# A graph layer's edge gather: 19 chunks loaded row by row from the sync engine, and gathers issued 17 instead of 26 ahead

## The chip, the cores and the metric

The kernel runs on one core of a Trainium2 chip. A core has five engines that run side by side, each through its own list of instructions in order: TensorE (PE in the profile: matmuls; PEld: its weight loads), VectorE (DVE), ScalarE (ACT), GpSimd (POOL) and SyncE (SP). They wait for each other by semaphores. DMA transfers are issued by an engine's sequencer (SP, ACT) or by POOL, and run on 16 DMA engines. SP does no arithmetic: here it issues DMAs and loads registers.

The metric is the device time of one execution in microseconds (us). The kernel before was timed in three runs.

## The reference

A pre-norm graph layer over 12500 nodes of 128 values and 200000 edges, of which the rows `dst` are sorted:

```python
h = jnp.maximum(_layernorm(x, axis=-1), 0.0)
msgs = z[src]                                        # z is h: 200000 rows of 128
agg = jax.ops.segment_sum(msgs, dst, num_segments=n)
deg = jax.ops.segment_sum(jnp.ones((src.shape[0],), z.dtype), dst, num_segments=n)
agg = agg / jnp.maximum(deg, 1.0)[:, None]
h = jax.nn.relu(agg @ Wg + z @ Ws + bg)
h = jnp.tanh(h @ W1 + b1)                            # 128 -> 512
h = jnp.tanh(h @ W2 + b2)                            # 512 -> 512
return h @ W3 + b3                                   # and x is added
```

So for each edge a row of 512 bytes has to be fetched from the normalized table by a number known only at run time, and the rows of edges with the same destination have to be summed.

## The kernel before

**Tables.** A first stage normalizes x and leaves the result twice: in HBM as `htab` (a row a node) and in SBUF, transposed, as `tab` (a column a node). The edges are cut into 1563 chunks of 128. A chunk is summed by one matmul: the 128 fetched rows are the weights, a one-hot matrix of 24 columns (`oh`, made on DVE by `onehot`, line 541) says which destination each row belongs to, and the result is added into a PSUM bank `agg` (or `edge`, for chunks across two blocks of nodes). Float32 matmuls stand in the trace as two records each. After each block of 512 nodes the layer's dense part (`h`, `w`, `pm`) runs on PE and ACT, in pieces between the chunks.

**Four sources of a chunk's rows.**

- *Raw*: ten groups of 8 chunks (`raw`, line 102) are gathered from x itself at the very start, before `htab` is there, by 80 indirect DMAs of POOL (line 217), and normalized later on DVE.
- *Gathered*: 1323 chunks are fetched by one indirect DMA each, issued by POOL (`gather`, line 455), into the pool `rows_in` of AHEAD = 26 buffers. Gather number j + 26 goes into the buffer of number j, so POOL waits there until PE has used chunk number j.
- *ACT's pairs*: 72 chunks (`column_copies`, line 492) are put together in SBUF by ACT: 64 small instructions a chunk, each combining two columns of `tab`, addressed by registers that a TENSOR_LOAD fills from the table `places` (16 at a time). PE then transposes the result (`turn`, line 511) and ACT copies it to `turned`.
- *DVE's pairs*: 88 chunks, in the same way on DVE (`column_pairs`, line 501).

Which chunk goes to whom is set in lines 128 to 139: every fourth chunk (3, 7, 11, ...) from 30 on that is not raw is a slot, and slots are dealt out by shares (SHARES, ENDS), each claimant gathering a fraction of a slot at each step, from a starting credit of 0.5.

**Order.** The program is written out chunk by chunk (line 918 on) in one order for all engines. `behind` counts the gathered chunks passed so far. `load_times` gives, in that count, where pieces of ACT's and DVE's loads are written. SP's list holds, in program order: the loads of `nearby` (98 windows of destination bytes, one each 14 chunks, written 5 windows ahead of their use in `tallied` on DVE; 6 buffers), the loads of x (`xb`, one a block) and the stores of the result. Further dependences (`last`, `newest`) keep DVE's pairs and tallies in the written order.

Of the kernel before, what the change touches and what calls it, by code (L numbers as in the profile page):

```python
# [22 lines left out]
F32 = mybir.dt.float32  # L23
BF16 = mybir.dt.bfloat16
I32 = mybir.dt.int32
# [6 lines left out]
P = 128  # L32
# [5 lines left out]
NRAW = 10  # L38
RAW0 = 256
STEP = 112  # L40
AHEAD = 26
LATE, SOON = 28, 14
LEAD = 24
QUICK = 1312
# [36 lines left out]
def windowed(ctx, tc, x, src, dst, Wg, Ws, bg, W1, b1, W2, b2, W3, b3, out, flag):  # L81
# [46 lines left out]
    lanes = ([], [])  # L128
    slots = [c for c in range(AT, NCH, EVERY) if FROM <= c < max(ENDS) and not raw(c)]
    within = [sum(c < end for c in slots) for end in ENDS]  # L130
    owed = [0.5] * 3
    for c in slots:
        shares = [n / k * (c < end) for n, k, end in zip(SHARES, within, ENDS)]
        owed = [o + n for o, n in zip(owed, [*shares, 1 - sum(shares)])]
        kind = max(range(3), key=lambda k: owed[k])
        owed[kind] -= 1
        if kind < 2:
            lanes[kind].append(c)
    apart = sum(lanes, [])

# [101 lines left out]
    places = const.tile([NROW, CPR // EVERY, P], I32, name="places")  # L242
# [39 lines left out]
    with tc.tile_pool(name="ln", bufs=2) as ln:  # L282

        def indices(name, a, pad, keep):
# [7 lines left out]
            nc.scalar.dma_start(r[FULL : FULL + 1, :REST], a[FULL * ROW : E].rearrange("(p e) -> p e", p=1))  # L292
            if name == "src":
                some = r.rearrange("r (q p) -> r q p", p=P)[:, AT::EVERY]
                nc.vector.tensor_scalar(
                    places.rearrange("r q (i t) -> r q t i", t=2), some.rearrange("r q (t i) -> r q t i", t=2),
                    4.0, float(TAB_AT), op0=ALU.mult, op1=ALU.add,
                )
            else:
                r8 = sp.tile([NROW, ROW], U8, name="r8")  # L300
                nc.scalar.copy(r8, r.bitcast(U8).rearrange("r (e b) -> r e b", b=4)[:, :, 0])
                end = ahead_of + NROW * ROW
                nc.scalar.dma_start(bytes_at[ahead_of:end].rearrange("(r e) -> r e", e=ROW), r8)
                past = sp.tile([1, max(ahead_of, past_end)], U8, name="past")
                nc.vector.memset(past, PAST)
                nc.scalar.dma_start(bytes_at[:ahead_of].rearrange("(o e) -> o e", o=1), past[:, :ahead_of])
                nc.scalar.dma_start(bytes_at[end:].rearrange("(o e) -> o e", o=1), past[:, :past_end])
# [144 lines left out]
    def sp_dma(*a):  # L452
        tc.keep_in_program_order(nc.sync.dma_start(*a))
# [8 lines left out]


    def offsets(lane, c, p0):
        r, q = divmod(c, CPR)
        kind = (mybir.EngineType.Activation, mybir.EngineType.DVE)[lane]
        loads, vs = nc.values_load_multi_w_load_instructions(  # L467
            places[r : r + 1, q // EVERY, p0 : p0 + LOADS], engines=[kind], min_val=TAB_AT,
            max_val=TAB_AT + (N - 1) * 4,
            skip_runtime_bounds_check_because="src holds rows of x, as the indirect DMAs take it to",  # L470
        )
        for ld in loads:
            if lane and last:
# [5 lines left out]
        vs = [v.with_bounds(min_val=TAB_AT, max_val=TAB_AT + (N - 1) * 4, guaranteed_mod_val=0, out_of_modulus=4) for v in vs]  # L479
        return enumerate(vs, p0)  # L480

    columns, last = {}, []

    def two(lane, c, p0):

        by_pair = columns[c].rearrange("p (t i) -> p i t", t=2)
        at_v = dict(offsets(lane, c, p0))
        for p in range(p0, p0 + LOADS, 2):
            a, b = (tab[:, bass.ds((at_v[q] - TAB_AT) // 4, 1)] for q in (p, p + 1))
            yield p, by_pair[:, p // 2], a, b  # L490

    def column_copies():
        for c in lanes[0]:
            columns[c] = ed.tile([P, P], F32, name="cols1", bufs=4)
            for p0 in range(0, P, LOADS):
                for p, to, a, b in two(0, c, p0):
                    act.activation(to, both_first, AF.Identity, bias=b, scale=a)
                    if (p + 2) % TOGETHER == 0:
                        yield

    def column_pairs():
        for c in lanes[1]:
            columns[c] = ed.tile([P, P], F32, name="cols2", bufs=6)
            for p0 in range(0, P, LOADS):
                for p, to, a, b in two(1, c, p0):
                    last[:] = [tc.keep_in_program_order(nc.vector.scalar_tensor_tensor(  # L506
                        to, first_only, a, b.to_broadcast([P, 2]), op0=ALU.mult, op1=ALU.subtract
                    ))]
                yield

    def turn(c):

        pt, both = ps_m.tile([P, 4, P], F32, name="pm"), columns.pop(c)
        pe.transpose(pt[:, 0, :], both, ident)
        r = ed.tile([P, D], F32, name="turned", bufs=6)
        act.activation(r, pt[:, 0, :], AF.Copy, scale=-1.0 if c in lanes[0] else 1.0)
        rows_t[c] = r


# [21 lines left out]
    def onehot(g):  # L541
        k = min(GRP, NCH - g * GRP)
        is_raw = raw(g * GRP)
        w = W_RAW if is_raw else W
        oh = ed.tile([P, GRP, W_RAW], F32, name="ohr", bufs=1) if is_raw else oh_bufs[g % OHS]
        newest[:] = [nc.vector.tensor_tensor(  # L546
            oh[:, :k, :w], lane[:, None, :w].to_broadcast([P, k, w]),
            dloc[:, g * GRP : g * GRP + k][:, :, None].to_broadcast([P, k, w]), op=ALU.is_equal,
        )]
        for c in range(g * GRP, g * GRP + k):  # L550
            if c in lanes[0] or c in lanes[1]:
# [217 lines left out]

    def costs(b):  # L770
        n = blocks[b][1]
        return n, 4 * (n / 2400 + 0.003), 0.5 + n / 1200 + (BEHIND if at < lanes[0][-1] else 0)

    def wide(b):

# [100 lines left out]
    def load_times(lane):  # L876
        use = [sum(o < c for o in order) for c in lanes[lane]]
        if not use:
            return
        step = (use[-1] - use[0]) // max(1, len(use) - 1)  # L880
        use = [max(FROM - 46 + MARGIN, use[0] - step), *use]
        some = LOADS if lane else TOGETHER
        for i in range(len(lanes[lane])):
            for k in range(P // some):
                yield max(FROM - 30, use[i] + (use[i + 1] - use[i]) * k * some // P - (MARGIN + GRP if lane else MARGIN))

    loading = [
        (loads, list(load_times(i))) for i, loads in enumerate((column_copies(), column_pairs()))
    ]
    turns = sorted((max(1, sum(o < c for o in order) - MARGIN // 2), c) for c in apart)  # L890
    work, done, nxt, behind = [], 0, 0, 0
    ngrp = -(-NCH // GRP)
    now = at = 0
# [24 lines left out]
    for c in range(NCH):  # L918
# [12 lines left out]
                factors(stats_raw)  # L931

        if c % (GRP // 2) == 0 and g + 2 < ngrp:
            copies, times = loading[1]
            while times and times[0] <= behind:
                times.pop(0)
                next(copies, 0)
# [423 lines left out]
```

## Time and profile before

| | us |
|---|---|
| three runs | 1783.35, 1785.84, 1782.18; median 1783.35 |
| the profiled execution | 1784.42 |
| its span, first to last instruction | 1782.2 |
| POOL busy in the span | 1331.8 (75%) |
| ACT busy | 1538.4 (86%) |
| PE busy | 1387.7 (78%) |
| DVE busy | 1177.0 (66%) |

Busy shares don't count the register, branch, semaphore and DMA-issuing instructions of an engine's sequencer, so SP has no busy time at all, and an engine can be behind without being at 100%. The waits are read by what ended an idle stretch ("<-"); a wait put down to "issue" is one for which the profile shows no semaphore.

### The profile page before, as it was taken

The page shows a single profiled execution, that of the slowest core. Times are in us where ns is not written, and L with a number is a line of the kernel's source. Part 1 is how long each engine was busy: PE and PEld are TensorE (multiplying, and loading weights), DVE is VectorE, ACT ScalarE, POOL GpSimd, SP SyncE. Part 2 cuts the span into 40 slices and gives each one's busy share as a digit, 9 for nine tenths or more (in the row PEclk, how much of TensorE's full clock was granted, in tenths as well). Part 3 has the DMA queues.
Part 4 walks back from the last instruction along what each step waited for, and adds up shares of the span by engine and source line. Part 5 has one row for each costly group of instructions (what it writes and reads, how often), then busy time and mean ns, then how long its engine had stood idle before and what let it go on. Part 6 is the DMA issues. An engine that isn't in the chain of part 4 may idle for free.

```text
span 1782.2 us, 27816 instructions
## 1 busy us (share of the span) xinstructions
PE 1387.7 (78%) x5426; PEld 927.2 (52%) x5426; DVE 1177.0 (66%) x6620; ACT 1538.4 (86%) x5189; POOL 1331.8 (75%) x1412
## 2 busy tenths in 40 slices
PE   1345554799798887878888888888898899879897
PEld 1334444466465555545555545555555555555577
DVE  7979987786567767567575766667757567565200
ACT  2478977999999999999899999999999999996222
POOL 7777777777777777777777777777777777777774
PEclk9999999866877887887776888778786788888898
DMA  8832222222222222222222222222222222222221
GB/s 206 238 91 56 56 56 66 68 60 72 58 73 70 71 62 70 72 59 70 71 60 70 73 60 69 73 59 71 71 60 70 71 57 73 71 66 71 59 63 38
DMA packets 116384, 131.36 MB, mean 74 GB/s; under 512 B 29463, under 2 KB 92819, under 8 KB 116008
## 3 DMA queue, kind: packets, MB, share of 16 engines
q0 software_dynamic: 44896, 92.04, 19.9%
q1 hardware_dynamic: 68030, 33.94, 7.1%
q10 hardware_dynamic: 3276, 3.51, 0.7%
q14 instruction: 136, 1.11, 0.2%
q8 instruction: 46, 0.75, 0.2%
HBM read 116.37 MB, written 13.03 MB: 73 GB/s over the span
## 4 chain that ended last, share of the span: by engine, by line
PE 29%; ACT 25%; DMA 20%; issue 10%; DVE 6%; ACTq 4%; POOL 3%; DVEq 0%; POOLq 0%
ACT cols L524 22%; DMA rows<-htab,scol 20%; PE pm L447 19%; PE agg L447 6%; ACTq L467 4%; DVE cols L506 3%; POOL rows L457 3%; ACT h L524 2%; PE edge L447 2%; PE pm L450 1%; DVE h L280 1%; DVEq L467 0%; ACT turned L524 0%; PE pm L385 0%; DVE nearby L593 0%
## 5 line engine op out<-in xcount | busy, mean ns | idle before, releaser
L457 POOL DMA_INDIRECT rows<-htab,scol x1323 | 1252.7, 947 | 403.2 <-issue 214.6
L524 ACT ACTIVATE cols<-both_first,tab 128x2 f32<-128x2 f32 x4608 | 1337.4, 420 | 11.9 <-issue 8.0
L506 DVE SCALAR_TENSOR_TENSOR cols<-first_only,tab 128x2 f32<-128x2 f32 x5632 | 813.0, 217 | 284.9 <-issue 283.5
L447 PE MATMUL pm<-h,w 128*128 128x512 f32 (+4 forms) x1344 | 792.8, 691 | 33.7 <-ACT h L524 20.6
L447 PEld LDWEIGHTS agg<-oh,rows 128*128 128x128 f32 x1910 | 393.3, 255 | 411.5 <-DMA rows<-htab,scol 224.9
L447 PE MATMUL agg<-oh,rows 128*128 128x24 f32 x1910 | 392.1, 306 | 169.9 <-DMA rows<-htab,scol 149.7
L447 PEld LDWEIGHTS pm<-h,w 128*128 128x128 f32 x1344 | 245.3, 231 | 42.8 <-ACT h L524 21.8
L447 PEld LDWEIGHTS edge<-oh,rows 128*128 128x128 f32 x736 | 136.7, 228 | 158.5 <-DMA rows<-htab,scol 77.4
L447 PE MATMUL edge<-oh,rows 128*128 128x24 f32 x736 | 136.9, 283 | 63.7 <-DMA rows<-htab,scol 51.3
L546 DVE TENSOR_TENSOR oh<-shared,dloc 128x192 f32<-128x192 f32 x186 | 65.0, 350 | 171.2 <-PE agg L447 95.1
L524 ACT ACTIVATE h<-pm,b2c 128x512 f32<-128x512 f32 (+4 forms) x112 | 72.8, 650 | 56.7 <-PE pm L447 56.6
L217 POOL DMA_INDIRECT raw<-in_x_dram,rsrc x80 | 78.2, 977 | 25.8 <-issue 24.1
L524 ACT ACTIVATE h<-pm,b1c 128x512 f32<-128x512 f32 (+4 forms) x112 | 71.7, 651 | 19.0 <-PE pm L447 18.8
L593 DVE TENSOR_SCALAR_CACHE_REDUCE nearby<-nearby,parity 128x656 uint8<-128x656 uint8 x98 | 86.5, 883 | 0.0
L385 PE MATMUL pm<-ident,h 128*128 128x128 f32 x98 | 23.5, 424 | 66.5 <-DVE h L280 54.0
L447 PEld LDWEIGHTS agg<-oh,turned 128*128 128x128 f32 x214 | 49.5, 258 | 45.5 <-issue 42.1
L450 PE MATMUL pm<-ident,cols 128*128 128x128 f32 x160 | 57.8, 361 | 14.2 <-ACT turned L524 6.2
L524 ACT ACTIVATE turned<-pm 128x128 f32<-128x128 f32 x160 | 48.2, 301 | 21.1 <-PE pm L450 21.0
L450 PEld LDWEIGHTS pm<-ident,cols 128*128 128x128 f32 x160 | 40.8, 255 | 29.3 <-ACT turned L524 9.6
L385 PEld LDWEIGHTS pm<-ident,h 128*128 128x128 f32 x98 | 19.4, 224 | 70.2 <-ACT sq L270 25.9
L746 DVE TENSOR_TENSOR mT<-agg,sums 128x136 f32<-128x136 f32 (+6 forms) x57 | 15.2, 269 | 61.4 <-PE agg L447 55.6
L447 PE MATMUL pm<-ident,h 128*128 128x128 f32 (+1 forms) x196 | 45.2, 318 | 8.8 <-ACT h L524 8.7
(129 smaller groups left out, 812.3 us busy)
## 6 DMA issues: line engine op xcount, KB each, us to landing
rows<-htab,scol POOLq DMA_INDIRECT x1323
nearby<-bytes_at SPq DMA_DIRECT2D x98, 82.0 KB, 2.3
xb<-in_x_dram SPq DMA_DIRECT2D x23, 256.0 KB, 3.3
out_dram<-o SPq DMA_DIRECT2D x23, 256.0 KB, 2.5
xt<-in_x_dram SPq DMA_DIRECT2D x8, 640.0 KB, 5.9
htab<-h SPq DMA_DIRECT2D x8, 640.0 KB, 4.4
raw<-in_x_dram,rsrc POOLq DMA_INDIRECT x80
w<-in_L_gnn_W_dram ACTq DMA_DIRECT2D x1, 1024.0 KB
```

The lines of the kernel that those rows point to most:

```text
L217: nc.gpsimd.indirect_dma_start(out=t[:, j, :], out_offset=None, in_=x, in_offset=bass.IndirectOffsetOnAxis(ap=rsrc[:, g, j : j + 1], axis=0),)
L280: nc.vector.scalar_tensor_tensor(h, xt, 0.0, spread(stats[:, 1], k), op0=ALU.max, op1=ALU.mult)
L385: nc.tensor.transpose(p[:, t, :], h[:, a + t, :], ident)
L447: tc.keep_in_program_order(nc.tensor.matmul(*a, **k))
L450: tc.keep_in_program_order(nc.tensor.transpose(*a, **k))
L457: nc.gpsimd.indirect_dma_start(out=r, out_offset=None, in_=htab, in_offset=bass.IndirectOffsetOnAxis(ap=scol[:, c : c + 1], axis=0),)
L467: loads, vs = nc.values_load_multi_w_load_instructions(places[r : r + 1, q // EVERY, p0 : p0 + LOADS], engines=[kind], min_val=TAB_AT, max ...
L506: last[:] = [tc.keep_in_program_order(nc.vector.scalar_tensor_tensor(to, first_only, a, b.to_broadcast([P, 2]), op0=ALU.mult, op1=ALU.subtract
L524: tc.keep_in_program_order(nc.scalar.activation(*a, **k))
L546: newest[:] = [nc.vector.tensor_tensor(oh[:, :k, :w], lane[:, None, :w].to_broadcast([P, k, w]), dloc[:, g * GRP : g * GRP + k][:, :, None ...
L593: done = nc.vector.tensor_scalar(w, w, parity[:, t % 2 : t % 2 + 1], None, op0=ALU.is_equal, op1=ALU.add, accum_out=found[:, t : t + 1])
L746: nc.vector.tensor_tensor(out, s, t, op=ALU.add)
```

## The change

A fourth kind of chunk is added. SP loads the 128 rows of a chunk by 128 DMAs of 512 bytes from `htab` into a pool of 4 buffers (`rows_one`; the tiles are called `srows`). The addresses come from a second table, `place0`, with the byte offset of each row, made by one more DVE instruction in the first stage; SP fills 32 registers by one TENSOR_LOAD and issues 32 DMAs from them. No transpose is needed: `srows` has the form that `rows` has. AHEAD goes from 26 to 17.

```diff
-AHEAD = 26
+AHEAD = 17
-SHARES = 72, 88
-FROM, ENDS = 30, (1480, 1540)
+SHARES = 20, 72, 88
+FROM, ENDS = 30, (1500, 1480, 1540)
+SBUFS = 4
-LOADS = 16
+LOADS = 32, 16, 16
...
-    owed = [0.5] * 3
+    owed = [-0.5, 0.5, 0.5, 0.5]
...
+    rows_one = ctx.enter_context(tc.tile_pool(name="rows_one", bufs=SBUFS))
...
+                nc.vector.tensor_scalar(places[0], some, float(ROWB), None, op0=ALU.mult)
...
+    hbytes = htab.rearrange("n d -> (n d)").bitcast(U8)
...
+    def row_loads(lane):
+        for c in lanes[lane]:
+            r = rows_one.tile([P, D], F32, name="srows")
+            rows_t[c] = r
+            rb = r.bitcast(U8)
+            for p0 in range(0, P, LOADS[0]):
+                for p, v in offsets(lane, c, p0):
+                    sp_dma(rb[p : p + 1, :], hbytes[bass.ds(v, ROWB)].rearrange("(o b) -> o b", o=1))
+                    if (p + 1) % TOGETHER == 0:
+                        yield
...
-        use = [max(FROM - 46 + MARGIN, use[0] - step), *use]
-        some = LOADS if lane else TOGETHER
+        use = [max(FROM - 46 + MARGIN, use[0] - step), *use] if lane else [use[0] - step * k for k in range(SBUFS - 1, 0, -1)] + use
+        if lane == 0:
+            use = [max(u, FROM // 2 + 7 * step // 8 * i) for i, u in enumerate(use)]
+        some = LOADS[2] if lane == 2 else TOGETHER
...
-            copies, times = loading[0]
-            while times and times[0] <= behind:
-                times.pop(0)
-                next(copies, 0)
+            for rows_of_lane, times in loading[:2]:
+                while times and times[0] <= behind:
+                    times.pop(0)
+                    next(rows_of_lane, 0)
```

With a starting credit of -0.5 the share of 20 comes to 19 chunks by the dealing rule: 119, 175, 255, 323, 403, 479, 559, 627, 715, 775, 855, 939, 995, 1083, 1151, 1223, 1307, 1379 and 1439. ACT keeps 72 and DVE 88, of other slots than before in part. Counted in gathered chunks (`behind`), the 19 are used at 108, 157, 227, 279, 342, 408, 471, 523, 593, 645, 708, 774, 823, 893, 952, 1008, 1074, 1137 and 1189, and chunk number i of them is loaded from the i-th to the next of these places: 15, 67, 119, 171, 223, 275, 327, 379, 431, 483, 535, 593, 645, 708, 774, 823, 893, 952, 1008 and 1074.

On POOL, from the last two raw groups to the end of the kernel's main part, the list before is the following (`raw` are the gathers from x, `rows` those from `htab`):

```order
L217 DMA raw_173<-in_x_dram,rsrc 128x128 x8
L217 DMA raw_182<-in_x_dram,rsrc 128x128 x8
L457 DMA rows<-htab,scol 128x128 x1323
L1326 TENSOR_LOAD flag
L1327 COMPARE_AND_BRANCH
```

and of the change:

```order
L219 DMA raw_176<-in_x_dram,rsrc 128x128 x8
L219 DMA raw_185<-in_x_dram,rsrc 128x128 x8
L462 DMA rows<-htab,scol 128x128 x1304
L1346 TENSOR_LOAD flag
L1347 COMPARE_AND_BRANCH
```

Only the count of gathers from `htab` differs, by 19; eight raw groups stand ahead of these rows in both.

On SP, at the start of the loop over chunks, the list before is (`begins` are the places of the `nearby` windows, `xb` rows of x):

```order
L579 TENSOR_LOAD begins
L453 DMA nearby<-bytes_at 128x656 x14
L579 TENSOR_LOAD begins
L453 DMA nearby<-bytes_at 128x656 x3
L453 DMA xb<-in_x_dram 128x4x128
L453 DMA nearby<-bytes_at 128x656 x5
```

and of the change:

```order
L597 TENSOR_LOAD begins
L458 DMA nearby<-bytes_at 128x656 x6
L473 TENSOR_LOAD place_204
L458 DMA srows<-htab 1x512 x8
L458 DMA nearby<-bytes_at 128x656
L458 DMA srows<-htab 1x512 x24
L473 TENSOR_LOAD place_204
L458 DMA srows<-htab 1x512 x8
L458 DMA nearby<-bytes_at 128x656
L458 DMA srows<-htab 1x512 x24
```

From the seventh `nearby` load on, each stands behind some 32 row loads and a TENSOR_LOAD that were not there.

On PE, at the first raw group (chunk 256 on), the list before is (the operand behind the comma is the source of the chunk's rows, and `pm` are matmuls of the dense part):

```order
L447 MATMUL pm<-h_512_10214,w_657 128x512
L447 MATMUL edge<-oh_205,rows 128x24 x2
L447 MATMUL pm<-h_512_10214,w_657 128x512
L450 MATMUL pm<-ident,cols_10909 128x128
L447 MATMUL edge<-oh_205,rows 128x24
L447 MATMUL edge<-ohr,raw_101 128x160
```

and of the change:

```order
L452 MATMUL edge<-oh_209,rows 128x24 x2
L452 MATMUL pm<-h_512_11658,w_662 128x512
L452 MATMUL edge<-oh_209,rows 128x24 x2
L452 MATMUL pm<-h_512_11658,w_662 128x512
L452 MATMUL edge<-oh_209,srows 128x24
L452 MATMUL edge<-ohr,raw_104 128x160
```

The last chunk before the raw group, number 255, was gathered by POOL and now comes from SP's rows; it is summed by the same matmul at the same place.

More of the change, by code (lines that the diff above doesn't have):

```diff
@@ L134, in windowed @@
         owed = [o + n for o, n in zip(owed, [*shares, 1 - sum(shares)])]
-        kind = max(range(3), key=lambda k: owed[k])
+        kind = max(range(4), key=lambda k: owed[k])
         owed[kind] -= 1
-        if kind < 2:
+        if kind < 3:
             lanes[kind].append(c)
@@ L241, in windowed @@
     scol = const.tile([P, NCOL], I32, name="scol")
-    places = const.tile([NROW, CPR // EVERY, P], I32, name="places")
+    ROWB = 4 * D
+    places = [const.tile([NROW, CPR // EVERY, P], I32, name=f"place{i}") for i in range(2)]
     dloc = const.tile([P, NCOL], F32, name="dloc")
@@ L294, in indices @@
                 some = r.rearrange("r (q p) -> r q p", p=P)[:, AT::EVERY]
+                nc.vector.tensor_scalar(places[0], some, float(ROWB), None, op0=ALU.mult)
                 nc.vector.tensor_scalar(
-                    places.rearrange("r q (i t) -> r q t i", t=2), some.rearrange("r q (t i) -> r q t i", t=2),
+                    places[1].rearrange("r q (i t) -> r q t i", t=2), some.rearrange("r q (t i) -> r q t i", t=2),
                     4.0, float(TAB_AT), op0=ALU.mult, op1=ALU.add,
@@ L464, in offsets @@
     def offsets(lane, c, p0):
+        step, first_at = (4, TAB_AT) if lane else (ROWB, 0)
         r, q = divmod(c, CPR)
-        kind = (mybir.EngineType.Activation, mybir.EngineType.DVE)[lane]
+        kind = (mybir.EngineType.SP, mybir.EngineType.Activation, mybir.EngineType.DVE)[lane]
         loads, vs = nc.values_load_multi_w_load_instructions(
-            places[r : r + 1, q // EVERY, p0 : p0 + LOADS], engines=[kind], min_val=TAB_AT,
-            max_val=TAB_AT + (N - 1) * 4,
+            places[min(lane, 1)][r : r + 1, q // EVERY, p0 : p0 + LOADS[lane]], engines=[kind], min_val=first_at,
+            max_val=first_at + (N - 1) * step,
             skip_runtime_bounds_check_because="src holds rows of x, as the indirect DMAs take it to",
@@ L472, in offsets @@
         for ld in loads:
-            if lane and last:
+            if lane == 2 and last:
                 tc.add_manual_dep(
@@ L478, in offsets @@
             tc.keep_in_program_order(ld)
-        vs = [v.with_bounds(min_val=TAB_AT, max_val=TAB_AT + (N - 1) * 4, guaranteed_mod_val=0, out_of_modulus=4) for v in vs]
+        if lane:
+            vs = [v.with_bounds(min_val=first_at, max_val=first_at + (N - 1) * step, guaranteed_mod_val=0, out_of_modulus=4) for v in vs]
         return enumerate(vs, p0)
+    def row_loads(lane):
[8 more added lines that the diff above has]
+                        yield
     columns, last = {}, []
@@ L487, in two @@
         at_v = dict(offsets(lane, c, p0))
-        for p in range(p0, p0 + LOADS, 2):
+        for p in range(p0, p0 + LOADS[lane], 2):
             a, b = (tab[:, bass.ds((at_v[q] - TAB_AT) // 4, 1)] for q in (p, p + 1))
@@ L492, in column_copies @@
     def column_copies():
-        for c in lanes[0]:
+        for c in lanes[1]:
             columns[c] = ed.tile([P, P], F32, name="cols1", bufs=4)
-            for p0 in range(0, P, LOADS):
-                for p, to, a, b in two(0, c, p0):
+            for p0 in range(0, P, LOADS[1]):
+                for p, to, a, b in two(1, c, p0):
                     act.activation(to, both_first, AF.Identity, bias=b, scale=a)
@@ L501, in column_pairs @@
     def column_pairs():
-        for c in lanes[1]:
+        for c in lanes[2]:
             columns[c] = ed.tile([P, P], F32, name="cols2", bufs=6)
-            for p0 in range(0, P, LOADS):
-                for p, to, a, b in two(1, c, p0):
+            for p0 in range(0, P, LOADS[2]):
+                for p, to, a, b in two(2, c, p0):
                     last[:] = [tc.keep_in_program_order(nc.vector.scalar_tensor_tensor(
@@ L515, in turn @@
         r = ed.tile([P, D], F32, name="turned", bufs=6)
[L516 removed]
+        act.activation(r, pt[:, 0, :], AF.Copy, scale=-1.0 if c in lanes[1] else 1.0)
         rows_t[c] = r
@@ L771, in costs @@
         n = blocks[b][1]
-        return n, 4 * (n / 2400 + 0.003), 0.5 + n / 1200 + (BEHIND if at < lanes[0][-1] else 0)
+        return n, 4 * (n / 2400 + 0.003), 0.5 + n / 1200 + (BEHIND if at < lanes[1][-1] else 0)
     def wide(b):
@@ L880, in load_times @@
         step = (use[-1] - use[0]) // max(1, len(use) - 1)
-        use = [max(FROM - 46 + MARGIN, use[0] - step), *use]
-        some = LOADS if lane else TOGETHER
+        use = [max(FROM - 46 + MARGIN, use[0] - step), *use] if lane else [use[0] - step * k for k in range(SBUFS - 1, 0, -1)] + use
+        if lane == 0:
+            use = [max(u, FROM // 2 + 7 * step // 8 * i) for i, u in enumerate(use)]
+        some = LOADS[2] if lane == 2 else TOGETHER
         for i in range(len(lanes[lane])):
             for k in range(P // some):
-                yield max(FROM - 30, use[i] + (use[i + 1] - use[i]) * k * some // P - (MARGIN + GRP if lane else MARGIN))
+                yield max(FROM - 30 if lane else 1, use[i] + (use[i + 1] - use[i]) * k * some // P - (0, MARGIN, MARGIN + GRP)[lane])
     loading = [
-        (loads, list(load_times(i))) for i, loads in enumerate((column_copies(), column_pairs()))
+        (loads, list(load_times(i))) for i, loads in enumerate((row_loads(0), column_copies(), column_pairs()))
     ]
-    turns = sorted((max(1, sum(o < c for o in order) - MARGIN // 2), c) for c in apart)
+    turns = sorted((max(1, sum(o < c for o in order) - MARGIN // 2), c) for c in sum(lanes[1:], []))
     work, done, nxt, behind = [], 0, 0, 0
```

6 lines of the change are left out of this document (3 added, 3 removed).

## The prediction

> **What bounds the kernel now.** The page's first lines say only that several engines are busy, ACT most of all:
>
> ```profile
> span 1782.2 us, 27816 instructions
> PE 1387.7 (78%) x5426; PEld 927.2 (52%) x5426; DVE 1177.0 (66%) x6620; ACT 1538.4 (86%) x5189; POOL 1331.8 (75%) x1412
> ```
>
> POOL's 75% misleads. The waits of POOL alone, then POOL's order of time around the first gather from `htab`, then the gathers as one group:
>
> ```profile
> POOL rows L457 <- issue: 214.6, 704, 0.3
> POOL rows L457 <- DMA rows<-htab,scol: 80.1, 263, 0.3
> POOL rows L457 <- PE agg L447: 60.0, 197, 0.3
> ...
> 104.54 0.94 POOL L217 DMA_INDIRECT raw<-in_x_dram,rsrc  x1 [0.30 <-issue]
> 105.79 0.94 POOL L457 DMA_INDIRECT rows<-htab,scol  x1 [0.30 <-DVE begins L571]
> 107.03 0.94 POOL L457 DMA_INDIRECT rows<-htab,scol  x1 [0.30 <-issue]
> 108.28 0.94 POOL L457 DMA_INDIRECT rows<-htab,scol  x1 [0.30 <-issue]
> ...
> L457 POOL DMA_INDIRECT rows<-htab,scol x1323: 940/944/1845, 105.8 to 1760.5; - x189
> ```
>
> The last number of a wait is the longest one. No wait of POOL ahead of a gather is over 0.3 us, whatever it is put down to, and 0.30 stands ahead of those that wait for nothing too: it belongs to the gather. So POOL issues a gather each 0.94 + 0.30 = 1.25 us without a break, and the first gather from `htab` follows the last raw one with the same 0.30: POOL is not even held up by the first stage. 1323 gathers start from 105.8 to 1760.5, (1760.5 - 105.8) / 1322 = 1.252 us each. The span is 105.8 (nearly all raw gathers) + 1322 x 1.252 + 21.7 after the last start, in which the last block's dense part runs. **POOL's list is the bound from end to end**; PE follows it, as its waits say (the three longest for rows and for ACT):
>
> ```profile
> PE agg L447 <- DMA rows<-htab,scol: 149.7, 217, 2.3
> ...
> PE edge L447 <- DMA rows<-htab,scol: 51.3, 66, 2.0
> PE pm L447 <- ACT h L524: 32.4, 17, 4.8
> ```
>
> **The change, part by part.**
>
> *19 gathers fewer.* POOL's list goes from 1323 to 1304: 19 x 1.252 = **-23.8 us**, if nothing else holds POOL up. What lies behind the last gather is the same.
>
> *17 buffers in place of 26.* POOL now waits if PE finishes with a chunk over 17 x 1.252 = 21.3 us after its gather started (32.5 before). How far behind was PE? The worst place that I found, by counting: POOL's gathers up to 339.5 us, and PE's matmuls on `rows` up to 357.1 us.
>
> ```profile
> L457 POOL DMA_INDIRECT rows<-htab,scol x185: 940/944/1845, 105.8 to 339.1; - x185
> ...
> L447 PE MATMUL agg<-oh,rows x278: 186/388/409, 108.3 to 357.1; 128*128 128x24 f32 x139
> L447 PE MATMUL edge<-oh,rows x94: 186/387/409, 174.2 to 341.2; 128*128 128x24 f32 x94
> ```
>
> Two records a chunk: 372 / 2 = 186 chunks, the last just begun, so the 185th gather, started at 339.1, was used up by 357.0, after 17.9 us. Two of SP's chunks (119 and 175) come ahead of that place, so POOL is there 2.5 us earlier; if PE doesn't get earlier at all, the distance is 20.4, still under 21.3. I take 0 for the buffers, and 2 us for such places together.
>
> *SP's new work.* Does SP get through? A row load costs SP its register move and its DMA instruction. The trace has no register-addressed one-row load. Nearest are two one-row DMAs back to back on ACT's queue, and SP's six 128-row register-addressed loads at the start:
>
> ```profile
> 24.68 0.25 ACTq L306 DMA_DIRECT2D bytes_at<-past  x1
> 24.97 0.27 ACTq L307 DMA_DIRECT2D bytes_at<-past  x1
> ...
> 107.35 2.75 SPq L453 DMA_DIRECT2D nearby<-bytes_at  x6
> ...
> L453 SPq MOVE nearby<-bytes_at x98: 29/29/37, 107.3 to 1412.0; - x98
> ...
> L467 ACTq TENSOR_LOAD <-places x576: 1006/1037/1764, 96.6 to 1623.2; - x192
> L579 SPq TENSOR_LOAD <-begins x7: 1169/1379/2915, 105.8 to 1224.7; - x7
> ```
>
> The one-row pair starts 0.29 apart; the six start (2.75 - 0.38) / 5 = 0.47 apart, their move within it. So a row lies between 0.29 and 0.47; I take 0.29 + 0.03 for the move + as much for its gap = 0.35, as it moves one row. For a TENSOR_LOAD of 32 registers I take two of ACT's 16-register ones, 2.1 us; the ends are one SP load of 14 at its shortest, 1.2, and two of its longest, 5.8. A chunk costs SP 128 x 0.35 + 4 x 2.1 = 53.2, and with it pass some 4.5 `nearby` loads, one `xb` and one store, 3.0 together: **56.2 us**. The first ten chunks are written 52 gathers apart, 52 x 1.252 = 65.1 us for each, the later ones 60 in the mean, 75 us. SP has 9 us to spare even at the closer step and stays early, so I cost it at nothing; a chunk is written to be complete 38 to 110 gathers (47 to 137 us) ahead of its use, which covers it. At the ends it is 128 x 0.29 + 4.8 + 3.0 = 45 and 128 x 0.47 + 23.2 + 3.0 = 86 us; the second is a rival below.
>
> Eight completion semaphores take turns on SP's DMAs, so a row's landing matters only if it takes over 8 x 0.35 = 2.8 us:
>
> ```profile
> nearby<-bytes_at SPq DMA_DIRECT2D x98, 82.0 KB, 2.3
> ```
>
> 2.3 / 8 = 0.29 a row, under the 0.35. The Trainium skill, page "DMA: Bandwidth & Descriptors", section "Rules for kernel authors", speaks against such loads: many small transfers should be put together, since under 64 KB one pays mostly overhead. Were that overhead paid in turn, a chunk would take 128 x 2.3 = 294 us and SP 19 x 294 = 5.6 ms; but the six `nearby` loads are issued within 2.75 us, little over one landing, so the trace shows the overhead overlapped, and only the issue is to be paid.
>
> *The second table.* One more DVE instruction of the size of this one:
>
> ```profile
> L295 DVE TENSOR_SCALAR places<-idx_raw x1: 619/619/619, 26.4 to 26.4; 98x512 int32<-98x512 int32 x1
> ```
>
> 0.6 us on DVE at 26 us. POOL's raw gathers run till 105.5 and cover it; bare it would be 0.6.
>
> *More traffic beside the gathers.* While SP's six loads (768 rows) were issued, from 107.35 to 110.1, POOL's gathers kept their 1.25 (107.03, 108.28 above). I take 0; there is no reason for a gain, and the other end is the third rival's price.
>
> *PE* gets the same matmuls, and 19 chunks need no new transpose. Its list moves as a whole.
>
> **Sum.** 1782.2 - 23.8 + 2 = 1760.4 of span; the profiled execution has 2.2 more than its span (1784.42), and stands 1.1 over the median of the runs, so 1784.4 - 21.8 = 1762.6, or 1761.5 against the median. I say **1762**.
>
> **The rivals.**
>
> *ACT takes over.* Three stretches of the span (time, then each engine's busy time), and ACT's longest wait:
>
> ```profile
> core 0: us, PE busy (x) PEld busy (x) DVE busy (x) ACT busy (x) POOL busy (x), PEclk, DMA share, GB/s
> 106.00:300.00 194.00, 106.82 (x374) 86.32 (x374) 166.95 (x793) 157.37 (x550) 147.69 (x153) 1.00 0.24 61
> 300.00:1500.00 1200.00, 1007.47 (x3789) 644.46 (x3787) 818.56 (x5015) 1179.08 (x4054) 907.12 (x962) 0.78 0.26 67
> 1500.00:1640.00 140.00, 118.19 (x485) 77.64 (x484) 84.85 (x550) 128.57 (x428) 105.87 (x113) 0.83 0.26 69
> ...
> ACT h L524 <- PE pm L447: 107.3, 71, 7.9
> ```
>
> From 300 to 1500 ACT is idle for 20.9 us of 1200. SP's chunks 175 to 1307, sixteen, fall there, so POOL wants that stretch 20.0 us shorter with ACT's work unchanged: ACT would be at 100%. Against it: ACT waits 107 us for PE's `pm`, where it is ahead and could give up some of that lead, and PE's own longest wait for ACT is 4.8 us, far under the 21.3 us by which PE may be late before POOL stops. A loss shows only once lead and buffers are used up. If none of ACT's idle time can be used, only the three other chunks pay: -3.8 us, 1779.6. Half of it used gives 1770.
>
> *SP becomes the bound, and it is slower.* If SP needs S us a chunk over the 65.1, it is 10 x (S - 65.1) late after ten chunks. `nearby` loads stand behind the rows; they are written 70 chunks ahead of `tallied`, 70 x (1760.5 - 105.8) / 1563 = 74 us. Then DVE stops, with the one-hot matrices behind it, then PE, and POOL some 21 - 4 = 17 us later: 91 us of cover. The gain is eaten from 10 x (S - 65.1) = 91 + 23.8 on, S = 76.6, that is 0.51 us a row with my other prices, or a landing over 8 x 0.51 = 4.1 us. At the upper end, S = 86, it costs 209 - 91 - 23.8 = +94: 1877. Against it: both dear prices are needed at once, as 0.47 a row alone gives S = 72.
>
> *The gathers themselves slow down.* If the 2432 row transfers lengthen a gather by 1.8% (1.252 to 1.270), 1304 x 0.018 = 23.8 us are gone and the time is the same, 1783. Or SP's rows are there but POOL's list isn't the bound after all. The steady 1.25 beside SP's bursts speaks against it.
>
> **Chances.** Forecast (1758 to 1768) 0.73; ACT takes over in part (1768 to 1780) 0.12; no change 0.05; slower through SP 0.10. A measurement can tell 0.2%, 3.6 us, from no change; the ACT case is still faster by that, but for its end. Faster 0.84, same 0.06, slower 0.10. The range reaches from 1757 (the lowest run, 1782.2, less 23.8, and a little) to 1779, ACT's whole price; only the SP case and the even one are left out.
>
> **What would show it.** POOL's gathers: 1304 from 105.8 to about 1737 at 1.25 us, no wait over 0.3, or a few of some us near 340 or 480. SP's row loads 0.35 apart, each chunk's last one landing 40 us or more before PE uses it. ACT's busy time from 300 to 1480 near 1180. I am wrong if POOL's waits on PE are long (ACT, or buffers), if DVE waits for `nearby`, or if the gathers' own step grows.

## The result, and the profile after

The change takes **1759.8 us** (median of four runs, 1758.43 to 1762.16) against 1783.51 (1782.18 to 1785.84) of the kernel before beside it: a ratio of 0.987 (95% interval 0.9852 to 0.9888), or 23.7 us less. The profiled execution of the change took 1762.16, the longest of the four, and has a span of 1760.0.

The page's first lines are almost those of before; nothing in the busy shares tells that 22 us of span went:

```profile
span 1760.0 us, 32780 instructions
PE 1354.0 (77%) x5426; PEld 912.6 (52%) x5426; DVE 1176.2 (67%) x6621; ACT 1536.1 (87%) x5189; POOL 1315.9 (75%) x1393
```

POOL's list again, as the gathers from `htab` in one group (shortest, median and longest duration in ns, first and last start in us):

```profile
L462 POOL DMA_INDIRECT rows<-htab,scol x1304: 940/944/1932, 106.6 to 1739.7; - x187
```

1304 gathers, (1739.7 - 106.6) / 1303 = 1.2533 us each, and 20.3 us behind the last start. From the span of before it is 19 gathers, -23.8; the first starts 0.8 later; 1303 steps at 1.2533 in place of 1.2516 cost 2.2; the tail is 1.4 shorter: -22.2, the whole difference.

The waits of POOL (total, count, longest):

```profile
POOL rows L462 <- issue: 209.8, 688, 0.3
POOL rows L462 <- PE agg L452: 66.3, 215, 0.9
POOL rows L462 <- DMA rows<-htab,scol: 62.2, 204, 0.3
```

One kind of wait is now over the gather's own 0.3. POOL's order of time shows the longest:

```profile
358.29 0.94 POOL L462 DMA_INDIRECT rows<-htab,scol  x1 [0.30 <-issue]
360.11 0.94 POOL L462 DMA_INDIRECT rows<-htab,scol  x1 [0.87 <-PE agg L452]
```

At 360 us POOL met the chunk 17 gathers back that PE had only just used up: the 17 buffers were full, for 0.57 us (0.87 less the usual 0.30). Three gathers later there is one more such wait, of 0.2 us, and from then on they suffice.

SP's new work, as one tile's instructions, and beside it the loads of its registers:

```profile
L458 SPq MOVE srows<-htab x2432: 29/29/29, 113.5 to 1419.8; - x188
L458 SPq DMA_DIRECT2D srows<-htab x2432: 227/228/323, 113.6 to 1419.9; - x188
```

```profile
L473 SPq TENSOR_LOAD <-place x76: 1888/2177/2746, 111.5 to 1405.1; - x76
```

SP's order of time has six rows in a block, and SP's longest sum of waits from 113 to 1420 us, while it loads rows, shows what it does otherwise:

```profile
124.20 1.85 SPq L458 DMA_DIRECT2D srows<-htab  x6
```

```profile
SPq L458 <- ACT o L545: 111.6, 14, 15.6
```

The six start (1.85 - 0.23) / 5 = 0.324 apart, and SP stands for 111.6 us at stores of the result that are not ready (360.8 in the whole span, the rest behind its last row): it has time to spare. Its rows were never what PE waited for by more than 0.5 us in sum.

ACT, by the three stretches that the prediction shows of before:

```profile
core 0: us, PE busy (x) PEld busy (x) DVE busy (x) ACT busy (x) POOL busy (x), PEclk, DMA share, GB/s
106.00:300.00 194.00, 103.47 (x375) 85.10 (x376) 166.09 (x791) 161.32 (x566) 147.65 (x153) 0.51 0.23 60
300.00:1500.00 1200.00, 997.28 (x3868) 645.05 (x3866) 834.06 (x5113) 1197.56 (x4125) 906.47 (x961) 0.79 0.26 69
1500.00:1640.00 140.00, 119.67 (x484) 74.94 (x485) 74.46 (x489) 108.47 (x354) 105.86 (x113) 0.87 0.25 67
```

ACT is busy for 1197.56 of 1200 us in the middle (1179.08 before): its idle time there is used up. The granted clock is lower in the first stretch (0.51 against 1.00), yet POOL makes the same 153 gathers in it as before.

### The profile page after: what moved, and what is told of

It reads as the page before. It is cut to its first block, busy times and chain, and to the rows that moved or that the text cites. A ratio compares the mean times of both kernels' runs of the same rounds, so it can differ in the third digit from the quotient of the medians.

```text
span 1760.0 us, 32780 instructions
## 1 busy us (share of the span) xinstructions
PE 1354.0 (77%) x5426; PEld 912.6 (52%) x5426; DVE 1176.2 (67%) x6621; ACT 1536.1 (87%) x5189; POOL 1315.9 (75%) x1393
## 4 chain that ended last, share of the span: by engine, by line
ACT 56%; PE 12%; DMA 9%; ACTq 7%; issue 6%; POOL 6%; DVE 3%; DVEq 0%; POOLq 0%
ACT cols L542 49%; PE pm L452 9%; DMA rows<-htab,scol 9%; ACTq L473 7%; ACT h L542 5%; POOL raw L219 4%; PE agg L452 2%; DVE cols L524 2%; POOL rows L462 2%; ACT turned L542 1%; PE edge L452 1%; ACT o L545 0%; ACT rd L545 0%; PE pm L455 0%; DMA raw<-in_x_dram,rsrc 0%
## 5 line engine op out<-in xcount | busy, mean ns | idle before, releaser
L462 POOL DMA_INDIRECT rows<-htab,scol x1304 | 1235.9, 948 | 398.4 <-issue 209.8
L542 ACT ACTIVATE cols<-both_first,tab 128x2 f32<-128x2 f32 x4608 | 1360.3, 506 | 7.5 <-issue 3.9
L452 PEld LDWEIGHTS agg<-oh,rows 128*128 128x128 f32 x1878 | 385.0, 254 | 350.2 <-issue 170.5
L452 PE MATMUL agg<-oh,rows 128*128 128x24 f32 x1878 | 371.9, 301 | 121.3 <-DMA rows<-htab,scol 92.7
L452 PE MATMUL edge<-oh,rows 128*128 128x24 f32 x730 | 133.2, 278 | 53.7 <-DMA rows<-htab,scol 41.3
L564 DVE TENSOR_TENSOR oh<-shared,dloc 128x192 f32<-128x192 f32 x186 | 65.1, 350 | 144.8 <-PE agg L452 76.8
L542 ACT ACTIVATE h<-pm,b2c 128x512 f32<-128x512 f32 (+4 forms) x112 | 81.0, 724 | 48.8 <-PE pm L452 48.7
L542 ACT ACTIVATE h<-pm,b1c 128x512 f32<-128x512 f32 (+4 forms) x112 | 79.7, 728 | 17.2 <-PE pm L452 17.0
L542 ACT ACTIVATE turned<-pm 128x128 f32<-128x128 f32 x160 | 61.8, 386 | 15.9 <-PE pm L455 15.9
L452 PE MATMUL agg<-oh,turned 128*128 128x24 f32 x222 | 47.6, 297 | 7.1 <-ACT turned L542 5.2
```

Source lines behind the costliest of these rows:

```text
L452: tc.keep_in_program_order(nc.tensor.matmul(*a, **k))
L462: nc.gpsimd.indirect_dma_start(out=r, out_offset=None, in_=htab, in_offset=bass.IndirectOffsetOnAxis(ap=scol[:, c : c + 1], axis=0),)
L542: tc.keep_in_program_order(nc.scalar.activation(*a, **k))
L564: newest[:] = [nc.vector.tensor_tensor(oh[:, :k, :w], lane[:, None, :w].to_broadcast([P, k, w]), dloc[:, g * GRP : g * GRP + k][:, :, None ...
```

## The experiments

**Two conditions.** The runs of the experiments fell on four chips. On two of them the kernel before took 1783.77 and 1782.4 us (medians), as above; on the other two 2179.9 and 2202.75, and no run of either pair comes near the other pair. In the second condition single instructions last as long as ever (the median gather 0.947 us in e2 and 0.944 in e10, the median DMA of a row 0.228 in both), but the engines' streams have gaps for which the profile shows no semaphore: the idle time put down to "issue" ahead of DVE's pairs is 486.4 us in e1 against 283.5 before, and ahead of ACT's 90.1 against 8.0. The clearest sight is one kernel in both (e2 and e10 below are the same program). SP's order of time in e2, then in e10, at the same six `nearby` loads and first rows:

```profile
168.58 13.29 SPq L458 DMA_DIRECT2D nearby<-bytes_at  x6
186.77 9.81 SPq L458 DMA_DIRECT2D srows<-htab  x8
```

```profile
108.29 2.75 SPq L458 DMA_DIRECT2D nearby<-bytes_at  x6
113.14 3.07 SPq L458 DMA_DIRECT2D srows<-htab  x8
```

Six loads take 13.29 us instead of 2.75. So the ratios of e1 to e8 hold for the condition with gaps only, and the times that were expected of them, worked out from 1783 us, can't be set beside them; e9 to e12 were made in the condition that was predicted and measured. Three kernels were run in both.

### Fewer buffers alone (e1, condition with gaps)

```diff
-AHEAD = 26
+AHEAD = 17
```

(on the kernel before)

> The kernel before with 17 buffers for gathered rows and nothing else changed: 1323 gathers. Theory (POOL's list of gathers is the bound, and PE is never over 17.9 us behind a gather, under the 21.3 us that 17 buffers cover): the same time, 1783 to 1785 us, no wait of POOL over 0.3 us. Rival (fewer buffers cost part of what the gathers save): over 1787 us, with POOL's waits on PE over 0.3 us.

Measured: 2171.87 against 2179.9, ratio 0.9955 (0.9934 to 0.9977). POOL does meet full buffers here, as its waits on PE show (total, count, longest):

```profile
POOL rows L457 <- PE agg L447: 184.6, 140, 14.2
```

but the time doesn't grow: with gaps PE is the late one, up to 39.9 us behind the start of a gather against 17.9 in the profile of before, and holding POOL back costs nothing. That it took 8 us less was not explained. It says little on the condition without gaps, where POOL is the bound; there, the profile of the change itself (two waits over 0.3, the longer 0.87) is the better witness.

### The loads without their gain (e2 with gaps, e10 without)

SP loads its 19 chunks into `srows`, nobody reads them, and POOL gathers the 19 as well: 1323 gathers, as before.

```diff
-    apart = sum(lanes, [])
+    apart = sum(lanes[1:], [])
...
             r = rows_one.tile([P, D], F32, name="srows")
-            rows_t[c] = r
```

> SP loads the rows of the 19 chunks as in the change, but POOL gathers these chunks too, and the gathered rows are used: 1323 gathers, 2432 row loads that nobody reads. Theory (only the count of gathers matters; SP's work and traffic lie beside them): 1782 to 1786 us, gathers 1.25 us apart. Rival (the row transfers slow the gathers): over 1787 us; a gather lengthened by 1 per cent gives 1800 us. Other rival (the gain comes from something else in the rewritten order): near 1760 us.

Measured with gaps: 2314.78 against 2179.9, ratio 1.0624 (1.0579 to 1.0669).

> SP loads the 19 chunks' rows, POOL gathers these chunks as well. If the kernel before takes about 1783 us here: 1782 to 1786 (traffic and SP's work are free, only the count of gathers matters), over 1787 if they are not. If it takes about 2190 us: 20 to 60 us over the change in the same call, as the 19 gathers more cost at least 24 us there, and the change itself is slower than the kernel before.

Measured without gaps: 1785.44 against 1783.77, ratio 1.0006 (0.9995 to 1.0017). Its gathers as a group:

```profile
L462 POOL DMA_INDIRECT rows<-htab,scol x1323: 940/944/1977, 105.1 to 1761.4; - x189
```

(1761.4 - 105.1) / 1322 = 1.253 each, and no wait over 0.3. All of the change is there but the 19 gathers fewer (and PE's use of `srows`), and all of the gain is gone. So the 2432 row transfers, SP's work, the second table and the 17 buffers cost nothing that can be measured, and the count of the gathers makes the gain.

With gaps the same loads cost 135 us. The waits of DVE there name the way:

```profile
DVE nearby L610 <- DMA nearby<-bytes_at: 341.4, 45, 20.7
```

SP spent 82 to 107 us on a chunk's loads (19 of them from 186.8 to 2001), where the list gives it 65 to 75 us at POOL's best pace; the `nearby` windows behind the rows came late, then what DVE makes behind them (PE waits 134.9 us in sum for `mT` alone), then PE, then POOL. That is the rival "SP becomes the bound", on a chip where its price is met.

### The gathers gone and no loads (e3, condition with gaps)

The 19 chunks get one tile of zeros, so their edges are missing from the sums.

```diff
-            r = rows_one.tile([P, D], F32, name="srows")
-            rows_t[c] = r
...
+    for c in lanes[0]:
+        rows_t[c] = no_rows
```

> The 19 chunks are neither gathered nor loaded by SP; PE sums a constant tile of zeros for them (their edges are missing from the result). 1304 gathers. Theory: as the change, 1757 to 1763 us, since SP's loads cost nothing where they are. Rival (the row loads or their traffic cost something that is hidden in the gain): below 1755 us.

Measured: 2142.02 against 2179.9, ratio 0.9816 (0.9775 to 0.9857). Against e1, which has 17 buffers too, it is 29.9 us less. The gathers lie (2106.9 - 162.4) / 1303 = 1.49 apart here, by this row:

```profile
L461 POOL DMA_INDIRECT rows<-htab,scol x1304: 938/944/1927, 162.4 to 2106.9; - x187
```

and 19 x 1.49 = 28.3. So with gaps too the kernel with fewer gathers is the faster one, by about their own length, and it is the loads that cost. As POOL also waits for PE there (175.3 us in sum), the agreement of the two numbers does not prove that the gathers' length is what was saved. It was not run without gaps.

### Each row loaded twice (e4), every second one (e5 with gaps, e12 without)

```diff
                     sp_dma(rb[p : p + 1, :], hbytes[bass.ds(v, ROWB)].rearrange("(o b) -> o b", o=1))
+                    sp_dma(spare_rows[p : p + 1, :], hbytes[bass.ds(v, ROWB)].rearrange("(o b) -> o b", o=1))
```

in e4, and in e5 and e12 with `if p % 2:` ahead of the added line.

> The change with each of the 2432 rows loaded twice, the second time into a spare tile that nobody reads. A chunk then costs SP 256 x 0.324 + 4 x 2.17 + 3.0 = 94.6 us, at 65 us steps at first and 75 later. Theory (SP's cover of about 91 us is used up and SP's list becomes the bound): 2000 to 2150 us, PE and DVE waiting for nearby loads or SP's rows, POOL for PE. Rival (issue of rows overlaps and is not what SP is limited by): within 10 us of 1760.

Measured with gaps, in two runs: 3000.81 against 2179.9, ratio 1.3756 (1.3688 to 1.3823).

> The change with every second row loaded twice, into a spare tile: 3648 row loads. A chunk costs SP 192 x 0.324 + 4 x 2.17 + 3.0 = 73.9 us; at steps of 65 us SP is late by 88 us after ten chunks, at later steps of 75 us no more. Theory (91 us of cover): within 5 us of the change, 1758 to 1766. Rival (less cover, the 74 us of the nearby loads or less, since DVE runs ahead): 1770 to 1800 us, with DVE or PE waiting for SP's DMAs.

Measured with gaps, on another chip: 2647.69 against 2202.75, ratio 1.2015 (1.1975 to 1.2054). SP needed 95.5 us a chunk in e2 (first to last row, by 19), 113.8 in e5 and 132.5 in e4, and the time was 135, 445 and 821 us over the kernel before: some 17 to 20 us more for each us more a chunk. There are 19 chunks, so this is what one expects where SP decides and each of them pays in full; SP's pace is taken as it ran, its own waits included, so the slope alone does not say who leads.

> Every second row loaded twice, once more: a chunk costs SP 73.9 us, late by 88 us after ten chunks at steps of 65 us. If the kernel before takes about 1783 us here: theory (91 us of cover): 1758 to 1766 us; rival (74 us of cover or less): 1770 to 1800 us, with DVE or PE waiting for SP's DMAs. If it takes about 2190 us: near 2650 as before.

Measured without gaps: 1841.17 against 1782.4, ratio 1.0341 (1.031 to 1.0373), above what either side expected. Its rows from SP:

```profile
L458 SPq DMA_DIRECT2D srows<-htab x2432: 227/228/386, 112.6 to 1589.1; - x188
```

(1589.1 - 112.6) / 19 = 77.7 us a chunk, for 73.9 expected. DVE first waits for a `nearby` window at 615, and POOL runs on till 779, 670 us from its first gather, without a wait that counts; then comes its first long one. In their orders of time, DVE's two waits, then PE's and POOL's:

```profile
615.30 0.90 DVE L615 TENSOR_SCALAR_CACHE_REDUCE nearby<-nearby,parity 128x656 uint8<-128x656 uint8 x1 [4.98 <-DMA nearby<-bytes_at]
...
788.99 0.90 DVE L615 TENSOR_SCALAR_CACHE_REDUCE nearby<-nearby,parity 128x656 uint8<-128x656 uint8 x1 [10.56 <-DMA nearby<-bytes_at]
```

```profile
791.23 2.07 PE L452 MATMUL pm<-mT,wg 128*128 128x512 f32 x2 [17.86 <-DVE mT L770]
...
779.19 0.95 POOL L462 DMA_INDIRECT rows<-htab,scol  x1 [0.30 <-issue]
793.83 0.94 POOL L462 DMA_INDIRECT rows<-htab,scol  x1 [13.69 <-PE agg L452]
```

DVE waits for a `nearby` window until 788.99, PE until 791.23 for `mT`, which DVE makes behind it (for the dense part; the rival had named the one-hot matrices), and POOL goes on at 793.83: the chain of the rival, link by link. By the starts of its chunks against the list's places at 1.252 us a gather, SP was 92 us late with the chunk begun at 738.3 and 107 us with the next, begun at 817.7.

POOL's longest wait of all has another cause. In SP's, PE's and POOL's orders of time:

```profile
1592.76 0.39 SPq L458 DMA_DIRECT2D xb<-in_x_dram  x1
...
1595.86 0.77 PE L452 MATMUL pm<-xb,ident 128*128 128x128 f32 x2 [28.80 <-DMA xb<-in_x_dram]
...
1600.03 0.94 POOL L462 DMA_INDIRECT rows<-htab,scol  x1 [26.19 <-PE agg L452]
```

A load of x, which PE needs for the block's result, stands in SP's list behind the last rows (the last one issued at 1589); PE waits 28.80 us for it, and POOL 26.19 for PE. In the change the same load is issued 50 us ahead of its use (at 1454.4, used at 1504.2), and PE waits nowhere for `xb`.

### Other shares (e7 with gaps, e11 without; e8)

```diff
-SHARES = 20, 72, 88
+SHARES = 25, 66, 98
```

in e7 and e11 (ACT gets fewer chunks, DVE and SP more; 1295 gathers), `25, 72, 98` in e8 (1288 gathers).

> Shares 25, 66, 98: SP loads 24 chunks, ACT makes 66, DVE 98; 1295 gathers. Theory (gathers are the bound as long as ACT, now with 6 chunks less, is not): 1759.8 - 9 x 1.25 = 1748.5, 1746 to 1753 us, ACT below 99 per cent busy between 300 and 1500 us. Rival (SP, with chunks every 48 gathers, or DVE takes over): over 1757 us.

Measured with gaps: 2480.68 against 2202.75, ratio 1.1273 (1.123 to 1.1316).

> Shares 25, 72, 98: SP loads 25 chunks, ACT keeps 72, DVE makes 98; 1288 gathers. If gathers alone were the bound: 1759.8 - 16 x 1.25 = 1739.8 us. Theory (ACT has 2.4 us of idle time left in the change between 300 and 1500 us, so it takes over, with 6 chunks more than in the kernel of shares 25, 66, 98): 1746 to 1760 us, POOL waiting on PE. Rival (ACT's busy time at 99.8 per cent is not its limit): 1737 to 1743 us.

Measured with gaps: 2479.47, ratio 1.1268 (1.123 to 1.1305). The two agree although ACT's share differs by six chunks: SP decides in both, as in e2 (DVE waits 435 and 464 us in sum for `nearby` windows), and nothing is learned of ACT.

> Shares 25, 66, 98 once more: SP loads 24 chunks, ACT makes 66, DVE 98; 1295 gathers. If the kernel before takes about 1783 us here: theory (gathers are the bound, ACT relieved of 6 chunks is not): 1760 - 9 x 1.25 = 1749, 1746 to 1753 us, ACT idle for more than the 2.4 us that it has in the change between 300 and 1500 us; rival (SP, with a chunk every 48 gathers at 53 us each, or DVE takes over): over 1757 us. If the kernel before takes about 2190 us: near 2480 as before.

Measured without gaps: 1768.31 against 1782.4, ratio 0.9921 (0.9901 to 0.9941). Nine gathers fewer than the change should be 11 us faster; it is 8 us slower than the change was in e9. ACT did get air, by the middle stretch of the three (columns as above):

```profile
300.00:1500.00 1200.00, 1005.96 (x3859) 643.25 (x3878) 895.99 (x5579) 1123.82 (x3836) 899.96 (x955) 0.79 0.26 69
```

and it bought nothing. The loss lies between 240 and 340 us, in POOL's order of time:

```profile
252.58 0.94 POOL L462 DMA_INDIRECT rows<-htab,scol  x1 [3.80 <-PE agg L452]
...
325.40 0.94 POOL L462 DMA_INDIRECT rows<-htab,scol  x1 [0.31 <-issue]
334.62 0.94 POOL L462 DMA_INDIRECT rows<-htab,scol  x1 [8.28 <-PE agg L452]
```

and what PE and POOL wait for from 230 to 350 us, in e11 and then in the change, with the wait of PE just ahead of POOL's longest between them:

```profile
PE agg L452 <- DVE oh L564: 30.8, 6, 8.0
POOL rows L462 <- PE agg L452: 24.3, 24, 8.3
```

```profile
331.60 2.07 PE L452 MATMUL pm<-mT,wg 128*128 128x512 f32 x2 [13.89 <-DVE mT L766]
```

```profile
PE agg L452 <- DVE oh L564: 13.4, 5, 6.4
POOL rows L462 <- PE agg L452: 6.4, 21, 0.3
```

There DVE normalizes the raw groups, tallies the first windows, and makes its own pairs. With more pairs it falls behind: it comes to its 13th tally of a window at 335.3 us in e11 and at 318.0 in the change, after 832 instructions of its pairs instead of 736. PE waits 17 us more in sum for one-hot matrices of `agg` (4 us less for those of `edge`) and 2 us more for `mT`, and 17 buffers do not cover it. SP's five chunks more are not the cause, as DVE has no wait for a `nearby` window in e11. That DVE's ten chunks more are is read from these times; a deal that spares DVE only in this stretch was not tried.

### Thirteen ahead (e6, condition with gaps)

```diff
-AHEAD = 17
+AHEAD = 13
```

> The change with 13 buffers instead of 17, 16.3 us of cover for PE's lateness. In the trace of the change some 40 gathers of 1304 are used up over 16.3 us late, at most 21.7. Theory (POOL loses about what the worst place of each late stretch goes over, once): 1765 to 1772 us. Rival (PE has slack and the loss is won back, the buffers do not matter): 1758 to 1763 us. Rival (each late gather is paid): over 1780 us.

Measured: 2294.93 against 2202.75, ratio 1.0427 (1.0394 to 1.046). Inconclusive: with gaps SP's loads decide (94.5 us a chunk), and the nearest run with 17 is e2, on another chip and with 19 gathers more. What 13 would cost without gaps was not tried.

### The change once more (e9, without gaps)

> The change itself once more, beside the kernel before on the same chip. In the runs of the experiments so far the kernel before took 2180 and 2203 us, not 1783, with the same instruction durations and gaps of 0.7 us and more on every engine's instruction stream. Theory A (where instruction streams have such gaps, SP's 5000 more instructions cost more than 19 gathers save): if the kernel before takes about 2190 us here, the change takes 2240 to 2310 us; if it takes 1783, the change takes 1757 to 1763. Rival B (the change saves its 19 gathers in either condition): 24 us or more below the kernel before in both.

Measured: 1760.36 against 1783.77, ratio 0.9881 (0.9864 to 0.9897), 23.4 us less, with no wait of POOL over 0.3 us this time. Beside e10, on the same chip, it is 25.1 us: the 19 gathers (23.8), and little else.

No kernel that was run without gaps is faster than the change.

## Why the prediction was right, point by point

1762 was predicted, 1759.8 measured.

- **POOL's list is the bound.** Right, and shown: with the 19 gathers put back (e10) the time is that of before; without them (e9) it is 23.4 us shorter, for 23.8 worked out.
- **17 buffers, 2 us.** The term was too large: the waits are 0.8 us together in the profiled run and were absent in e9. The place was right (the worst one was put at 339 us, and the two waits are for chunks gathered at 338 and 342), and so was the distance: PE was 21.7 us late there, 20.6 in e9, against 20.4 forecast and 21.3 allowed. That the forecast is 2.2 us off can't be put down to this term alone, as the four runs of the change lie 3.7 us apart. The buffers only just do: with DVE's part made later (e11), POOL's steps of over 1.5 us add up to 21.4 us beyond the usual 1.25, against 4.8 in e9.
- **SP's prices.** 0.324 a row for 0.35, 2.18 a register load for 2.1: 128 x 0.324 + 4 x 2.18 + 3.0 = 53.2 us a chunk, for 56.2. But SP did not stay early from the start, as the forecast had it: it stood for 57 us in sum at `nearby` loads that waited for DVE, and its third chunk, begun at 280.4, was 25 us behind the list's place. At 54 us a chunk it had made that up by the sixth. The chunk with the least to spare was the second, its last row issued 44.6 us ahead of PE's use of it, as PE was late there too; from the ninth on it is over 150 us (the later chunks are written up to 129 gathers ahead, not 110).
- **The dear small transfers.** The forecast set the rule on small transfers of the Trainium skill (page "DMA: Bandwidth & Descriptors", section "Rules for kernel authors") aside, since the overheads overlap. The trace agrees with the forecast: rows 0.324 apart, and 2432 of them cost nothing in e10.
- **The second table, the traffic.** Nothing, as forecast; both are in e10. The step of a gather went from 1.2516 to 1.2533 in the profiled run, 0.1% and not the rival's 1.8%.
- **ACT takes over.** ACT's idle time in the middle fell from 20.9 to 2.4 us, as the sum of this rival said, and still nothing was lost. PE's lead paid: the median time from a gather's start until PE has used its rows grew from 8.4 to 13.6 us for the gathers of 300 to 400 us, and from 8.6 to 11.9 for those of 400 to 500, nearly all within the buffers; from 1000 us on it is 4.0, as before. Not all of this comes with ACT's fuller list: e10, with 1323 gathers and ACT idle for 19 us in the middle, has 11.5 and 9.4. Its clock in the first stretch is 0.51 as in the change, and its order is the new one; which of the two makes PE later was not separated. The chain that ended last, followed back from the last instruction, now runs through ACT for more than half of the span:

```profile
ACT 56%; PE 12%; DMA 9%; ACTq 7%; issue 6%; POOL 6%; DVE 3%; DVEq 0%; POOLq 0%
```

  It had 25% before, and 40% in e9, the same kernel: the share moves much between executions of equal time. POOL, with next to no wait of its own, has 6%: two lists are now full side by side, and the chain follows the one that it met last. e11 shows that ACT alone isn't what is missing; how much further ACT's lateness could go is open.
- **SP becomes the bound.** The mechanism and its cover were right, and e12 shows them: DVE's first wait for a window, at 615, comes when SP begins its chunks 70 to 81 us late (74 were worked out), and POOL's first at 92 to 107 us (91 worked out). **The price was too kind.** By the prediction's formula a chunk of 77.7 us would cost 10 x 12.6 - 91 - 23.8 = 11 us over before; 58.8 were measured. Two terms are missing. The nine later steps were left out, but at 77.7 against 75 SP falls back further in them, 9 x 2.7 = 24 us; it begins its last chunk 147 us late. And the windows are not all that stands behind the rows in SP's list: the load of x for a block does too, and its lateness cost POOL 26 us at once. With both the sum is 11 + 24 + 26 = 61, for 58.8 measured. This is an estimate from one run; a kernel that issues `xb` earlier was not run. Without a late `xb` the even point lies where 10 x (S - 65.1) + 9 x (S - 75) = 91 + 23.8, at 75.8 us a chunk rather than 76.6; from which pace on `xb` costs was not measured.
- **What no step had.** That chips differ as in e1 to e8. The change itself was not run on a chip with gaps; e2 (1.0624, with 19 gathers more) makes it likely that it is slower than the kernel before there, by an estimate of 2314.78 - 28.3 against 2179.9, or 5%; e6, the change with 13 buffers, was 4% slower.

## What to carry to other kernels

Where one engine's list runs without a break, its length is the time, whatever the busy shares say. Work taken off it and given to an idle engine then saves its full length, if the buffers behind that list still cover the latest place of the others; look for that one place, not for an average. Price a new stream on an idle queue per item and against the *written* steps of the queue, all of them, with everything that stands behind it in line. And look at what else the list has to wait for before a further step of the same kind: here a deal with nine gathers fewer, and ten chunks more for DVE, met DVE's full list in a stretch of 100 us.

## What the runs showed of the hardware that was not expected

- The condition with gaps. The first gather from `htab` in e1, on a chip with gaps, in POOL's order of time:

```profile
102.47 0.95 POOL L217 DMA_INDIRECT raw<-in_x_dram,rsrc  x1 [0.30 <-issue]
164.01 0.94 POOL L457 DMA_INDIRECT rows<-htab,scol  x1 [60.60 <-DVE dloc L359]
```

  Without gaps nothing stood between them (105.79 before). By the start times of SP's instructions that wait for nothing, 379 gaps of over 0.4 us sum to 261 us in e2, and there is one, of 0.44 us, in e10, the same program without gaps; most are about 0.7 us. SP's loads, some 5000 instructions more, cost 135 us in e2 and nothing in e10. Durations of instructions are alike in both, so it looks as if instructions themselves arrive late; that was not tested, and the cause was not settled.
- A one-row DMA whose address is in a register costs SP's queue 0.228 us (0.324 with its move and gap), and the 128-row `nearby` load 0.33 (before) to 0.36 (the change): rows are a small part of the price of an issue.
- A TENSOR_LOAD costs more with more registers: 2.18 us for 32 on SP (median), 1.38 for 14 on SP, 1.04 for 16 on ACT; by how much, and how far the engines differ, was not measured apart.
